# A feed-forward product by Strassen's seven quarter products, with its sums on GpSimd and VectorE

## The chip, the cores and the metric

The kernel runs on one core of a Trainium2 chip. A core has five engines, each with its own instruction queue that it works through in order: TensorE (PE in the profile; PEld is its weight load), VectorE (DVE), ScalarE (ACT), GpSimd (POOL) and SyncE (SP, which here only issues DMAs). PE reads its two operands from the on-chip memory SBUF and writes into PSUM, eight banks of 128 partitions by 512 float32 columns; DVE and ACT read PSUM, POOL does not. Engines wait for each other through semaphores. The metric is the device time of one execution in microseconds (us), lower is better; the median of several runs is compared.

## What is computed

The reference is one layer of a small perceiver with 8 sequences of 64 tokens (512 tokens, width 512) in float32. Three blocks follow each other, each of them added to its input:

```python
x = x + xattn(layernorm(x), ctx)          # 1601 context rows per sequence
x = x + attn(layernorm(x), ...)           # causal linear attention, 16 heads of 64, and a feed-forward block
x = x + ffn(layernorm(x), ...)            # 8 experts, each token uses 2 of them
```

The second block is the one that the change touches. Its end, with `b` for the input of the block:

```python
num, den = causal sums of phi(q) phi(k) v  and  phi(q) phi(k)
a  = num / (den + 1e-6)
y  = b + a @ wo                                       # 1024 -> 512
h2 = ln(y, g2, beta2)
y  = y + gelu(h2 @ w1 + b1, approximate=False) @ w2 + b2   # 512 -> 2048 -> 512
```

## The kernel before, in words

The 512 tokens are held as NT = 4 tiles of 128, the width of 512 as KC = 4 chunks of 128, and the inner width FF = 2048 as 16 blocks f of 128. The order of the instructions on every engine is the order in which the program calls them: it is written out by hand, and nothing reorders it. A float32 matmul appears in the trace as two passes, each with its own weight load. An engine that needs something that another engine has not finished waits, and with it everything behind it in its queue.

Weights come through a ring of 12 buffers of 1 MB in one fixed order (`stream`, `need`): a call of `need` also lets SP issue the loads up to six places ahead, and marks older ring buffers as free. The buffers are filled again when their last reader is done. The order after the attention weights is wo (2), then w1 and w2 in turn (4 of each), then the experts' weights.

PSUM has two groups of four banks: `mm_bank` for short products and `acc_bank` for long accumulations. During the feed-forward block the four `acc` banks hold the four accumulators of the second product (`mlp_0` to `mlp_3`), so all the rest goes through the four `mm` banks. Accesses of one bank by different engines are put in order one after the other.

The last part of the linear attention runs over j, eight pairs of heads. `attend_j(j)` gives two banks, each with the numerators in its left half and the denominators in its right half. `divide(j)` (L768 to L780) has ACT copy the denominators of both banks into the tile `rden` (L772), DVE take the reciprocal (L773) and DVE multiply it with the numerators into `a_t` (L775). `rden` has one buffer.

`output(t, js)` (L800) is the product with wo, into one bank for each token tile t. `join(t)` adds it to the residual `xin` on DVE (L833) and takes the statistics (L835 to L839), `normal(t)` makes the normalized rows `h2n` (L844, L845), and `turn_h2(t)` transposes them on PE into one bank (L850); its four chunks are then scaled and shifted into `h2_t`, by DVE (L858) and ACT (L854) in turn. `h2n` and `h2_t` are the two halves of the tile `v_sb`, under which name the profile shows them. Tile 3 is ready last, since the order of PE places its wo product last.

The first product of the feed-forward block, `hidden(f, tokens)` (L887), takes four matmuls (one for each chunk of the width) with 128 columns of w1 as the weights and the tokens as the moving operand. For f = 0 and 1 it is first done for the tokens of tiles 0 to 2 alone, and `turn_h2(3)` stands between these two. After that the loop over f (L917 to L925) does one whole `hidden(f)` with 512 moving columns, one gelu on ACT from the bank into a tile `hid` (L921), and for f from 1 to 8 the second product `mlp_out` (L908) of the block before, four matmuls. The second product of the last HELD = 8 blocks comes later, one token tile after the other (`last_chunks`), and is interleaved with the routing for the experts.

Between `hidden(1, ...)` and the loop, POOL gets eight additions of 128x512, two for each token tile: b2 to `xin` (L902), then `xin` to the residual `xs` (L903). The results are first read when the second product of tile 0 is complete (L956).

Of the kernel before, what the change touches and what calls it, by code (L numbers as in the profile page):

```python
# [31 lines left out]
FF = 2048  # L32
# [7 lines left out]
HELD = 8  # L40
# [8 lines left out]
def perceiver_kernel(  # L49
# [22 lines left out]
    nc = tc.nc  # L72
# [29 lines left out]
    mid = ctx.enter_context(ExitStack())  # L102
# [15 lines left out]
    half = H * DH // 2  # L118
# [4 lines left out]
    streamed, order, issued = {}, [], [0]  # L123
# [59 lines left out]
    def issue_to(n):  # L183

        while issued[0] < min(n, len(order)):
            key, src = order[issued[0]]
            if in_ring(key) and len(held) >= RING:
                if held[0] not in freed:
                    return
                held.pop(0)  # L190
            if key in places_of:
                t_ = places_of[key]
                nc.sync.dma_start(t_, src)
            elif key[0] == "tail":
                t_ = tails.tile([P, D], F32, tag="tail", name="_".join(str(k) for k in key))
                nc.sync.dma_start(t_, src)
            else:
                width = WIDTHS[key[2]] if key[0] == "ctxT" else 512
                t_ = ring.tile([P, 4, width], F32, tag="ring", name="_".join(str(k) for k in key))
                nc.sync.dma_start(t_, src)  # L200
                held.append(key)
            streamed[key] = t_
            issued[0] += 1

    def done(*keys):

# [26 lines left out]
    g1_c, beta1_c, g2_c, beta2_c = (col[:, i * KC : (i + 1) * KC] for i in range(4))  # L233
    b1_c = col[:, 4 * KC : 4 * KC + FF // P]
# [431 lines left out]
    xas.close()  # L666


    las = ctx.enter_context(ExitStack())
    la1 = las.enter_context(tc.tile_pool(name="la1", bufs=1))  # L670
    la2 = las.enter_context(tc.tile_pool(name="la2", bufs=2))
    if True:
        a_t = la1.tile([P, H * DH // P, B * S], F32, name="a_t")

# [92 lines left out]

        def divide(j, both):  # L768

            rden = la2.tile([P, 2, NT * S], F32, tag="rden", bufs=1, name=f"rden_{j}")  # L770
            for h in range(2):
                nc.scalar.activation(rden[:, h, :], both[h][:, NT * S :], AF.Identity, bias=tiny)  # L772
            nc.vector.reciprocal(rden, rden)  # L773
            for h in range(2):
                nc.vector.tensor_tensor(  # L775
                    a_t[:, j, :].rearrange("p (t h q) -> p t h q", t=NT, h=2)[:, :, h, :],
                    both[h][:, : NT * S].rearrange("p (t q) -> p t q", t=NT),
                    rden[:, h, :].rearrange("p (t q) -> p t q", t=NT),
                    ALU.mult,
                )  # L780
# [12 lines left out]
        wo_r = [need("wo", r) for r in range(2)]  # L793
        wo_banks = {}

        def output(t, js):
            if t not in wo_banks:
                wo_banks[t] = (mm_bank if t < 3 else acc_bank)(f"wo_{t}")
            for j in js:
                nc.tensor.matmul(  # L800
                    wo_banks[t],
                    a_t[:, j, t * P : (t + 1) * P],
                    wo_r[j // 4][:, j % 4, :],
                    start=(j == 0),
                    stop=(j == nj - 1),
                )
# [22 lines left out]
        h2n, h2_t = v_sb[:, :, :D], v_sb[:, :, D:]  # L829
# [12 lines left out]
        def normal(t, mv, std):  # L842
            rstd = small.tile([P, 1], F32, tag="rstd1", name=f"rstd_h2_{t}")
            nc.vector.reciprocal(rstd, std)  # L844
            nc.vector.tensor_scalar(h2n[:, t, :], xin[:, t, :], mv[:, 0:1], rstd, ALU.subtract, ALU.mult)  # L845

        def turn_h2(t):
            bank = mm_bank(f"tr_h2_{t}")
            for c in range(KC):
                nc.tensor.transpose(bank[:, c * P : (c + 1) * P], h2n[:, t, c * P : (c + 1) * P], ident)  # L850
            for c in range(KC):
                dst, part = h2_t[:, c, t * P : (t + 1) * P], bank[:, c * P : (c + 1) * P]
                if c % 2:
                    nc.scalar.activation(  # L854
                        dst, part, AF.Identity, scale=g2_c[:, c : c + 1], bias=beta2_c[:, c : c + 1]
                    )
                else:
                    nc.vector.tensor_scalar(  # L858
                        dst, part, g2_c[:, c : c + 1], beta2_c[:, c : c + 1], ALU.mult, ALU.add
                    )  # L860

        of = join(0), join(1)
        for t in range(2):
# [17 lines left out]
    def hidden(f, tokens):  # L881

        w = need("w1", f // 4)
        if f not in hid_banks:
            hid_banks[f] = mm_bank(f"hid_{f}")
        for c in range(KC):
            nc.tensor.matmul(  # L887
                hid_banks[f][:, tokens],
                w[:, c, (f % 4) * P : (f % 4 + 1) * P],
                h2_t[:, c, tokens],  # L890
                start=(c == 0),
                stop=(c == KC - 1),
            )

    hid_banks = {}

    hidden(0, slice(0, 3 * P))
    turn_h2(3)
    hidden(1, slice(0, 3 * P))

    for t in range(NT):
        nc.gpsimd.tensor_tensor(xin[:, t, :], xin[:, t, :], b2_bc, ALU.add)  # L902
# [4 lines left out]
    def mlp_out(t, f, hid):  # L907
        nc.tensor.matmul(  # L908
            acc[t],
            hid[:, t * P : (t + 1) * P],  # L910
            need("w2", f // 4)[:, f % 4, :],
            start=(f == 0),
            stop=(f == FF // P - 1),
        )

    hids = []
    nf = FF // P  # L917
    for f in range(nf):
        hidden(f, slice(3 * P, 4 * P) if f < 2 else slice(0, 4 * P))
        hid = mlp2.tile([P, B * S], F32, tag="hid", bufs=HELD + 1, name=f"hid_sb_{f}")  # L920
        nc.scalar.activation(hid, hid_banks[f], AF.Gelu, bias=b1_c[:, f : f + 1])  # L921
        hids.append(hid)
        if 0 < f <= nf - HELD:
            for t in range(NT):
                mlp_out(t, f - 1, hids[f - 1])  # L925

    warm = mlp.tile([P, 1], F32, name="warm")
    nc.scalar.activation(warm, eps, AF.Sqrt)
# [174 lines left out]
    t = NT - 1  # L1103
# [51 lines left out]
    bank = acc_bank("counts")  # L1155
# [636 lines left out]
```

## The time and the profile before

| | |
|---|---|
| median of 3 runs | 631.76 us (631.12 to 632.06) |
| the profiled execution | 631.35 us, its span 629.5 us, 1.85 us around it |
| PE busy | 613.7 us, 97% of the span |
| DVE, ACT, POOL busy | 166.5, 136.1, 64.9 us |
| first product, L887 | 144 passes, 56.6 us busy |
| second product, L908 | 112 passes, 51.0 us busy |
| last wo product to first late chunk of the second product | 278.01 to 362.13 us |

The times in the views below are microseconds from the start of the span. A group's line gives the line in the kernel, engine, operation, output and inputs, the shape, the number of instructions, then their busy time in us and the mean duration of one in ns, then the engine's idle time just before them with what ended it. A line of the timeline gives the start, the length, the engine, the line, the operation, how many instructions were merged into it, and in brackets how long the engine sat idle before it and what released it. Matmuls overlap: the distance between the starts of two passes is what one costs, and is less than its duration.

### The profile page before, as it was taken

What the parts mean: (1) busy time and instruction counts of PE and PEld (TensorE: products, weight loads), DVE (VectorE), ACT (ScalarE), POOL (GpSimd) and SP (SyncE); (2) the same over time, 40 slices, a digit from 0 to 9 for tenths busy, and PEclk for the clock granted to TensorE, in tenths of its full rate; (3) what the DMA queues carried; (4) which work ended last, traced back from release to release, by engine and by line L of the source; (5) the groups of instructions that cost most, each with busy time, mean ns of one, the idle gap of its engine ahead of it and who ended that gap; (6) DMA issues with size and microseconds to landing.
All of it is one profiled execution on the core that took longest, in us unless ns stands there. A gap on an engine that the chain in (4) does not pass through costs nothing. (4 is left out here: it accounts for less than half of the span.)

```text
span 629.5 us, 8757 instructions
## 1 busy us (share of the span) xinstructions
PE 613.7 (97%) x3572; PEld 350.2 (56%) x3572; DVE 166.5 (26%) x398; ACT 136.1 (22%) x260; POOL 64.9 (10%) x89
## 2 busy tenths in 40 slices
PE   8999999999999999999999999999999999999994
PEld 6543534344444454445444447967783767775793
DVE  4112414242302757870000026511311101011100
ACT  2241232130134354231101111301101101111110
POOL 4000000000000000050000003331310121301110
PEclk9999999999999999999999999999999999999998
DMA  8999999999713004030312121437890577785711
GB/s 336 421 418 417 419 419 417 419 419 413 295 59 99 35 2 134 2 135 0 128 31 109 68 100 67 172 94 252 299 352 0 178 291 274 295 328 152 290 19 17
DMA packets 23937, 131.81 MB, mean 209 GB/s; under 512 B 4372, under 2 KB 4372, under 8 KB 12488
## 3 DMA queue, kind: packets, MB, share of 16 engines
q1 hardware_dynamic: 19496, 122.36, 49.6%
q0 software_dynamic: 3280, 7.61, 5.0%
q10 hardware_dynamic: 1104, 1.07, 0.5%
q8 instruction: 38, 0.62, 0.4%
q14 instruction: 19, 0.16, 0.1%
HBM read 126.08 MB, written 4.94 MB: 208 GB/s over the span
## 5 line engine op out<-in xcount | busy, mean ns | idle before, releaser
L1289 PEld LDWEIGHTS up<-xgT,e_up 128*128 128x128 f32 x896 | 100.7, 192 | 4.5 <-ACT y_sb L1267 2.5
L1289 PE MATMUL up<-xgT,e_up 128*128 128x128 f32 x896 | 101.6, 275 | 1.0 <-PEq L1622 0.6
L1303 PE MATMUL y<-e_wo,mid 128*128 128x512 f32 (+1 forms) x144 | 58.8, 547 | 0.0
L887 PE MATMUL hid<-v_sb,w 128*128 128x512 f32 (+2 forms) x144 | 56.6, 545 | 0.0
L1255 DVE TENSOR_TENSOR mid<-up,act 128x256 f32<-128x256 f32 x38 | 16.1, 425 | 150.3 <-ACT act L1253 150.3
L908 PE MATMUL mlp<-w,hid_sb 128*128 128x512 f32 x112 | 51.0, 597 | 0.0
L458 PE MATMUL sc<-ctxT,pw_t 128*64 128x401 f32 (+1 forms) x256 | 46.6, 503 | 0.3 <-DMA ctxT<-in_ctx_T_dram 0.3
L519 PE MATMUL av<-ctx,eT 128*64 128x512 f32 x192 | 44.3, 595 | 0.0
L887 PEld LDWEIGHTS hid<-v_sb,w 128*128 128x128 f32 x144 | 26.1, 190 | 29.2 <-issue 26.8
L1253 ACT ACTIVATE act<-up 128x256 f32<-128x256 f32 x38 | 14.6, 384 | 119.6 <-PE up L1289 97.4
L1303 PEld LDWEIGHTS y<-e_wo,mid 128*128 128x128 f32 x144 | 25.7, 190 | 20.5 <-issue 17.8
L1268 POOL DMA_INDIRECT out_dram<-y_sb,dst_late x12 | 18.3, 1526 | 167.4 <-ACT y_sb L1267 97.6
L908 PEld LDWEIGHTS mlp<-w,hid_sb 128*128 128x128 f32 x112 | 20.7, 190 | 23.5 <-issue 23.4
L458 PEld LDWEIGHTS sc<-ctxT,pw_t 128*64 128x64 f32 x256 | 17.6, 136 | 27.6 <-issue 26.3
L902 POOL TENSOR_TENSOR xin<-xin,b_bc 128x512 f32<-128x512 f32 x4 | 5.1, 1265 | 265.6 <-DVE rstd_h L844 262.7
L800 PE MATMUL wo<-wo,a_t 128*128 128x512 f32 x64 | 29.5, 603 | 1.1 <-DVE a_t L775 1.1
L684 PE MATMUL wq<-h_t,wq 128*128 128x512 f32 x64 | 29.4, 602 | 0.0
L589 PE MATMUL v<-wv,h_t 128*128 128x512 f32 x64 | 29.1, 597 | 0.0
L684 PE MATMUL wk<-h_t,wk 128*128 128x512 f32 x64 | 28.8, 592 | 0.0
L519 PEld LDWEIGHTS av<-ctx,eT 128*64 128x64 f32 x192 | 14.7, 136 | 25.1 <-issue 23.1
L773 DVE RECIPROCAL rden<-rden 128x512 f32<-128x512 f32 x8 | 26.8, 3346 | 1.5 <-ACT rden L772 1.5
L921 ACT ACTIVATE hid_sb<-hid,col 128x512 f32<-128x512 f32 x16 | 11.0, 687 | 68.0 <-PE hid L887 68.0
(272 smaller groups left out, 611.8 us busy)
## 6 DMA issues: line engine op xcount, KB each, us to landing
e_up<-in_L_ffn_up_dram SPq DMA_DIRECT2D x32, 1024.0 KB, 5.3
ctx<-in_ctx_dram SPq DMA_DIRECT2D x24, 1024.0 KB, 15.7
ctxT<-in_ctx_T_dram SPq DMA_DIRECT2D x24, 802.0 KB, 13.9
e_wo<-in_L_ffn_wo_dram SPq DMA_DIRECT2D x16, 1024.0 KB, 9.7
w<-in_L_attn_w_dram SPq DMA_DIRECT2D x8, 1024.0 KB, 8.7
ctxT<-in_ctx_T_dram SPq DMA_DIRECT2D x8, 796.0 KB, 17.6
wv<-in_L_attn_wv_dram SPq DMA_DIRECT2D x2, 1024.0 KB, 14.0
wq<-in_L_attn_wq_dram SPq DMA_DIRECT2D x2, 1024.0 KB, 15.6
```

Of the source, the lines that this page charges most:

```text
L458: nc.tensor.matmul(sc[h * S : (h + 1) * S, :width], pw_t[:, c, (2 * t + h) * S : (2 * t + h + 1) * S], keys[h][:, c, :], start=(c == 0), s ...
L519: nc.tensor.matmul(av[h * S : (h + 1) * S, :], e_t[:, 4 * g + j, h * S : (h + 1) * S], rows[h][:, j, :], start=(g == 0 and j == 0), stop=F ...
L589: nc.tensor.matmul(bank, h_t[:, c, t * P : (t + 1) * P], wv_n[:, c, :], start=(c == 0), stop=(c == KC - 1))
L684: nc.tensor.matmul(bank, w[:, c, (j % 4) * P : (j % 4 + 1) * P], h_t[:, c, :], start=(c == 0), stop=(c == KC - 1),)
L773: nc.vector.reciprocal(rden, rden)
L800: nc.tensor.matmul(wo_banks[t], a_t[:, j, t * P : (t + 1) * P], wo_r[j // 4][:, j % 4, :], start=(j == 0), stop=(j == nj - 1),)
L887: nc.tensor.matmul(hid_banks[f][:, tokens], w[:, c, (f % 4) * P : (f % 4 + 1) * P], h2_t[:, c, tokens], start=(c == 0), stop=(c == KC - 1),)
L908: nc.tensor.matmul(acc[t], hid[:, t * P : (t + 1) * P], need("w2", f // 4)[:, f % 4, :], start=(f == 0), stop=(f == FF // P - 1),)
L1255: nc.vector.tensor_tensor(hid, bank[:, FQ:], act, ALU.mult)
L1268: nc.gpsimd.indirect_dma_start(out=out, out_offset=bass.IndirectOffsetOnAxis(ap=dst[:n, :], axis=0), in_=y_sb[:n, :], in_offset=None, boun ...
L1289: nc.tensor.matmul(bank[:, m * P : (m + 1) * P], up_of[q][:, c, m * P : (m + 1) * P], xg_t[c], start=(c == 0), stop=(c == KC - 1),)
L1303: nc.tensor.matmul(bank[:, :width], h_t[:, j * P : (j + 1) * P], w[:, 2 * (q % 2) + j, n * width : (n + 1) * width], start=(q + j == 0), s ...
```

## The change

Three things change.

First, the first feed-forward product. Two blocks f = 2i and 2i+1, the two halves of the width (chunks 0, 1 and 2, 3) and the two halves of the tokens (tiles 0, 1 and 2, 3) make a product of 2 by 2 quarters. Strassen's form (Winograd's variant) takes seven quarter products in the place of eight, with four sums of weights (`sum_weights(i)`: s1 to s4, on POOL) and four sums of tokens (`sum_tokens`: t1 to t4, once; token tiles 0 and 2 on POOL, token tiles 1 and 3 on DVE). A quarter product is two matmuls with 256 moving columns. The seven results are put together partly by accumulating in a bank, partly by six DVE instructions for each i that read a bank, and three gelu activations in the place of two. `sum_weights(0)` and `(1)` are called ahead of the wo product, the others one round ahead of their use.

In a round i the instructions on PE are: P1 and P2 into bank 0 (P1 is copied out by DVE before P2 accumulates on it), P5 and P3 into bank 1, P6, P7 and P4 into bank 2, each of them with a DVE read between the products. P4 of round i is called one round later. Ahead of the loop PE does P1(0), P1(1), P2(0), P2(1), the transposes of tile 3, P1(2) and P2(2).

Second, `rden` gets two buffers.

Third, `turn_h2` lets one engine scale a whole bank: ACT for tiles 0 and 1, DVE for tile 2; tile 3 is transposed into two banks of the `acc` group, ACT scaling the one and DVE the other.

```diff
+    sumw = mid.enter_context(tc.tile_pool(name="sumw", bufs=2))
+    def quarter(i, row, half):
+        w = streamed["w1", i // 2]
+        at = (2 * (i % 2) + row) * P
+        return w[:, 2 * half : 2 * half + 2, at : at + P]
+    def sum_weights(i):
+        s = wsums[i] = sumw.tile([P, 4, 2, P], F32, tag="sumw", name=f"sumw_{i}")
+        s1, s2, s3, s4 = (s[:, k] for k in range(4))
+        nc.gpsimd.tensor_tensor(s1, quarter(i, 1, 0), quarter(i, 1, 1), ALU.add)
+        nc.gpsimd.tensor_tensor(s2, s1, quarter(i, 0, 0), ALU.subtract)
+        nc.gpsimd.tensor_tensor(s3, quarter(i, 0, 0), quarter(i, 1, 0), ALU.subtract)
+        nc.gpsimd.tensor_tensor(s4, quarter(i, 0, 1), s2, ALU.subtract)
...
-            rden = la2.tile([P, 2, NT * S], F32, tag="rden", bufs=1, name=f"rden_{j}")
+            rden = la2.tile([P, 2, NT * S], F32, tag="rden", name=f"rden_{j}")
...
         wo_r = [need("wo", r) for r in range(2)]
+        for i in range(2):
+            sum_weights(i)
...
+        def sum_tokens(eng, tile):
+            t1, t2, t3, t4 = (ts[:, :, tile * P : (tile + 1) * P] for ts in tsum)
+            near, far = tokens(0, 0, tile), tokens(0, 1, tile)
+            eng.tensor_tensor(t1, far, near, ALU.subtract)
+            eng.tensor_tensor(t3, tokens(1, 1, tile), far, ALU.subtract)
+            eng.tensor_tensor(t2, t3, near, ALU.add)
+            eng.tensor_tensor(t4, tokens(1, 0, tile), t2, ALU.subtract)
...
-        turn_h2(0)
-        turn_h2(1)
+        turn_h2(0, [by_act])
+        turn_h2(1, [by_act])
         output(3, range(3, nj - 2))
-        turn_h2(2)
+        turn_h2(2, [by_dve])
...
-    hidden(0, slice(0, 3 * P))
-    turn_h2(3)
-    hidden(1, slice(0, 3 * P))
+    def first_products(i):
+        need("w1", i // 2)
+        for f in range(2 * i, 2 * i + 2):
+            hids[f] = mlp2.tile([P, B * S], F32, tag="hid", bufs=HELD + 1, name=f"hid_sb_{f}")
+        open_bank(i, 0)
+        product(i, 1, 0, quarter(i, 0, 0), tokens(0, 0), True)
+        nc.vector.tensor_copy(hids[2 * i + 1][:, :HT], sides[i, 0][:, :HT])
+    def second_products(i):
+        product(i, 2, 0, quarter(i, 0, 1), tokens(1, 0))
+        gelu(2 * i, hids[2 * i][:, :HT], sides[i, 0][:, :HT])
+    def fifth(i):
+        open_bank(i, 1)
+        product(i, 5, 1, wsums[i][:, 0], tsum[0], True)
+        even, odd = hids[2 * i], hids[2 * i + 1]
+        nc.vector.tensor_tensor(odd[:, HT:], sides[i, 1][:, :HT], odd[:, :HT], ALU.add)
...
+    def fourth(i):
+        product(i, 4, 2, quarter(i, 1, 1), tsum[3])
+        odd = hids[2 * i + 1]
+        nc.vector.tensor_tensor(odd[:, :HT], sides[i, 2][:, :HT], odd[:, :HT], ALU.add)
+        gelu(2 * i + 1, odd, odd)
+    sum_tokens(nc.gpsimd, 0)
+    for i in range(2):
+        first_products(i)
+    for i in range(2):
+        second_products(i)
+    turn_h2(3, [by_act, by_dve])
+    sum_tokens(nc.vector, 1)
+    first_products(2)
+    second_products(2)
     for t in range(NT):
         nc.gpsimd.tensor_tensor(xin[:, t, :], xin[:, t, :], b2_bc, ALU.add)
         nc.gpsimd.tensor_tensor(xs[:, t, :], xs[:, t, :], xin[:, t, :], ALU.add)
...
+    np_ = nf // 2
+    for i in range(np_):
+        if i > 2:
+            first_products(i)
+        if i + 1 < np_ and i + 1 not in wsums:
+            sum_weights(i + 1)
+        fifth(i)
+        if i > 0:
+            fourth(i - 1)
+        sixth(i)
+        if i > 2:
+            second_products(i)
+        third(i)
+        seventh(i)
+        if 0 < i <= (nf - HELD) // 2:
+            for f in (2 * i - 2, 2 * i - 1):
+                for t in range(NT):
+                    mlp_out(t, f, hids[f])
+    fourth(np_ - 1)
```

`sixth`, `third` and `seventh` have the form of `fifth`: a product into the bank named above, then one DVE addition that reads it; `third` also has the gelu of the right half of block 2i.

More of the change, by code (lines that the diff above doesn't have):

```diff
@@ L671, in perceiver_kernel @@
     la2 = las.enter_context(tc.tile_pool(name="la2", bufs=2))
+    wsums = {}
+    def quarter(i, row, half):
[9 more added lines that the diff above has]
+        nc.gpsimd.tensor_tensor(s4, quarter(i, 0, 1), s2, ALU.subtract)
     if True:
@@ L845, in normal, with by_act @@
             nc.vector.tensor_scalar(h2n[:, t, :], xin[:, t, :], mv[:, 0:1], rstd, ALU.subtract, ALU.mult)
[L847 to L860, printed above, removed]
+        def by_act(dst, part, scale, shift):
+            nc.scalar.activation(dst, part, AF.Identity, scale=scale, bias=shift)
@@ new lines, in by_dve, with turn_h2 @@
+        def by_dve(dst, part, scale, shift):
+            nc.vector.tensor_scalar(dst, part, scale, shift, ALU.mult, ALU.add)
+        def turn_h2(t, scaled):
+            n = KC // len(scaled)
+            for i, scale in enumerate(scaled):
+                bank = (acc_bank if t == NT - 1 else mm_bank)(f"tr_h2_{t}_{i}")
+                for c in range(i * n, (i + 1) * n):
+                    part = bank[:, (c - i * n) * P : (c - i * n + 1) * P]
+                    nc.tensor.transpose(part, h2n[:, t, c * P : (c + 1) * P], ident)
+                for c in range(i * n, (i + 1) * n):
+                    part = bank[:, (c - i * n) * P : (c - i * n + 1) * P]
+                    scale(h2_t[:, c, t * P : (t + 1) * P], part, g2_c[:, c : c + 1], beta2_c[:, c : c + 1])
@@ new lines, in perceiver_kernel, with tokens @@
+        HT = B * S // 2
+        tsum = [h2n[:, k, :].rearrange("p (c q) -> p c q", c=2) for k in range(3)]
+        tsum.append(sumw.tile([P, 2, HT], F32, tag="sumh", bufs=1, name="sumh"))
+        def tokens(half, side, tile=None):
+            at = slice(side * HT, (side + 1) * HT) if tile is None else slice(side * HT + tile * P, side * HT + tile * P + P)
+            return h2_t[:, 2 * half : 2 * half + 2, at]
+        def sum_tokens(eng, tile):
[5 more added lines that the diff above has]
+            eng.tensor_tensor(t4, tokens(1, 0, tile), t2, ALU.subtract)
@@ L879, in perceiver_kernel @@
     mlp2 = mid.enter_context(tc.tile_pool(name="mlp2", bufs=2))
[L881 to L892, printed above, removed]
-            )
-    hid_banks = {}
@@ L897, in perceiver_kernel, with product @@
-    hidden(0, slice(0, 3 * P))
-    turn_h2(3)
-    hidden(1, slice(0, 3 * P))
+    sides, hids = {}, {}
+    nf = FF // P
+    def product(i, k, bank, weights, rows, first=False):
+        bank = sides[i, bank]
+        for c in range(2):
+            nc.tensor.matmul(
+                bank[:, :HT],
+                weights[:, c, :],
+                rows[:, c, :],
+                start=(first and c == 0),
+                stop=(c == 1),
+                skip_group_check=True,
+            )
@@ new lines, in open_bank, with gelu @@
+    def open_bank(i, k):
+        sides[i, k] = mm_bank(f"side_{i}_{k}")
+    def first_products(i):
[5 more added lines that the diff above has]
+        nc.vector.tensor_copy(hids[2 * i + 1][:, :HT], sides[i, 0][:, :HT])
+    def gelu(f, dst, src):
+        nc.scalar.activation(dst, src, AF.Gelu, bias=b1_c[:, f : f + 1])
@@ new lines, in second_products, with sixth @@
+    def second_products(i):
[6 more added lines that the diff above has]
+        nc.vector.tensor_tensor(odd[:, HT:], sides[i, 1][:, :HT], odd[:, :HT], ALU.add)
+    def sixth(i):
+        open_bank(i, 2)
+        product(i, 6, 2, wsums[i][:, 1], tsum[1], True)
+        even, odd = hids[2 * i], hids[2 * i + 1]
+        nc.vector.tensor_tensor(even[:, HT:], sides[i, 2][:, :HT], odd[:, :HT], ALU.add)
@@ new lines, in third, with seventh @@
+    def third(i):
+        product(i, 3, 1, wsums[i][:, 3], tokens(1, 1))
+        even = hids[2 * i][:, HT:]
+        nc.vector.tensor_tensor(even, sides[i, 1][:, :HT], even, ALU.add)
+        gelu(2 * i, even, even)
+    def seventh(i):
+        product(i, 7, 2, wsums[i][:, 2], tsum[2])
+        odd = hids[2 * i + 1]
+        nc.vector.tensor_tensor(odd[:, HT:], sides[i, 2][:, :HT], odd[:, HT:], ALU.add)
+    def fourth(i):
+        product(i, 4, 2, quarter(i, 1, 1), tsum[3])
+        odd = hids[2 * i + 1]
+        nc.vector.tensor_tensor(odd[:, :HT], sides[i, 2][:, :HT], odd[:, :HT], ALU.add)
+        gelu(2 * i + 1, odd, odd)
@@ L914, in mlp_out @@
         )
[L916 to L925, printed above, removed]
+    np_ = nf // 2
[17 more added lines that the diff above has]
+    fourth(np_ - 1)
     warm = mlp.tile([P, 1], F32, name="warm")
```

## The prediction

> **What bounds the kernel now.** I read the page's engine shares first, then the groups, then who waits for whom between 150 and 300 us, then the timeline around the change.
>
> ```profile
> PE 613.7 (97%) x3572; PEld 350.2 (56%) x3572; DVE 166.5 (26%) x398; ACT 136.1 (22%) x260; POOL 64.9 (10%) x89
> L887 PE MATMUL hid<-v_sb,w 128*128 128x512 f32 (+2 forms) x144 | 56.6, 545 | 0.0
> L908 PE MATMUL mlp<-w,hid_sb 128*128 128x512 f32 x112 | 51.0, 597 | 0.0
> ```
>
> TensorE is busy for 97% of the span: time goes only where PE passes go, or where a new wait makes PE idle. The waits of PE in this part are two:
>
> ```profile
> PE wo L800 <- DVE a_t L775: 1.1, 1, 1.1
> PE tr_h L850 <- DVE v_sb L845: 0.8, 1, 0.8
> ```
>
> The pitch of the passes, from the timeline (start, length, count):
>
> ```profile
> 338.10 24.20 PE L887 MATMUL hid<-v_sb,w 128*128 128x512 f32 x56
> ...
> 613.73 7.07 PE L1303 MATMUL y<-e_wo,mid 128*128 128x256 f32 x32
> ```
>
> A pass of 512 columns lasts 0.592 us (a group's mean) and 56 take 24.20, so the pitch is (24.20 - 0.592)/55 = 0.429 us. A pass of 256 lasts 0.379, and 32 take 7.07: pitch (7.07 - 0.379)/31 = 0.216. Halving the columns halves the price almost exactly; the weight load of 0.190 us still fits under it.
>
> **Part 1, passes.** Removed: 112 passes of 512 columns, 16 of 384 (8 take 2.74 us less the overlap, 0.32 each) and 16 of 128 (0.114): 112 x 0.429 + 16 x 0.32 + 16 x 0.114 = 48.0 + 5.1 + 1.8 = 55.0 us. Added: 8 rounds x 7 products x 2 matmuls x 2 passes = 224 passes x 0.216 = 48.3 us. Gain 6.7 us, all on PE's path. A check of the method: from 278.01 (the end of the wo product) to 362.13 (first late chunk) before has 55.0, 0.5 for four transposes, 64 passes of L908 x 0.429 = 27.5, and 0.8 idle: 83.8 of the measured 84.1.
>
> **Part 2, the denominators.**
>
> ```profile
> 255.17 0.84 ACT L772 ACTIVATE rden<-nd,tiny 128x256 f32<-128x256 f32 x2 [4.29 <-DVE a_t L775]
> 260.30 0.84 ACT L772 ACTIVATE rden<-nd,tiny 128x256 f32<-128x256 f32 x2 [4.29 <-DVE a_t L775]
> 261.17 3.35 DVE L773 RECIPROCAL rden<-rden 128x512 f32<-128x512 f32 x1 [0.99 <-ACT rden L772]
> ...
> 265.44 1.98 PE L800 MATMUL wo<-wo,a_t 128*128 128x512 f32 x4 [1.08 <-DVE a_t L775]
> ```
>
> ACT waits twice for the one buffer, so DVE sits idle 0.33 and 0.99 us before the last two reciprocals. With two buffers ACT has copied while DVE still divides; the last `a_t` comes 1.3 us earlier, more than PE's 1.08 us of waiting: gain 1.1, at least 0 (no work is added) and at most 1.1, since PE has no other idle time there.
>
> **Part 3, up to the first new products.** ACT alone scales tiles 0 and 1: eight of 0.405 (two take 0.81 in L854's rows), from about 273.3 to 276.6, before PE needs them at 278.01: 0. DVE is no longer held up by ACT in tile 2, so `join(3)` starts when its bank is complete, at 277.58 + 0.59 + 0.14 = 278.3 in the place of 278.74. `sum_weights(0)` and `(1)` are eight POOL additions of 256 columns, 0.75 us each by a line through 1.27 (512, L902) and 0.32 (32 columns, L291); POOL is idle from 8 to 270 us, so 0. The w1 loads are issued from 153 us on and land 5 to 13 us later. If that cover were gone, the 6 us would stand in front of P5(0).
>
> **Part 4, the first stall.** These are the rows before of tile 3's normalization:
>
> ```profile
> 270.69 1.58 DVE L845 TENSOR_SCALAR v_sb<-xin,mv_h,rstd_h 128x512 f32<-128x512 f32 x1
> 270.73 1.27 POOL L902 TENSOR_TENSOR xin<-xin,b_bc 128x512 f32<-128x512 f32 x1 [262.67 <-DVE rstd_h L844]
> 272.07 1.34 POOL L903 TENSOR_TENSOR xs<-xs,xin 128x512 f32<-128x512 f32 x1
> ...
> 278.74 0.68 DVE L833 TENSOR_TENSOR xin<-wo,xin 128x512 f32<-128x512 f32 x1
> ...
> 280.99 0.55 DVE L845 TENSOR_SCALAR v_sb<-xin,mv_h,rstd_h 128x512 f32<-128x512 f32 x1
> 281.59 0.66 PE L850 MATMUL tr_h<-ident,v_sb 128*128 128x128 f32 x4 [0.83 <-DVE v_sb L845]
> ```
>
> P2(0) accumulates on the bank that DVE's copy of P1(0) reads, and that copy is queued on DVE behind `join(3)` and `normal(3)`. From 278.3 the chain of 2.80 us (278.74 to 281.54) ends at 281.1; the copy takes 0.42 (256 columns, as L775). P2(0) starts at about 281.56. PE has only P1(0) and P1(1) before it: 278.01 + 8 x 0.216 = 279.74. Stall 1.8 us, where before it was 0.8. To this comes a wait that the first row shows: an L845 that met a POOL addition took 1.58 in the place of 0.55. After the change POOL is busy from 277.4 (when two chunks of tile 2 are scaled) with four sums, 3.0 us, and then eight additions of 1.3, up to 291, so `normal(3)` at 280.6 meets it for certain. Between 0 and 1.03 us more; I take 0.5.
>
> **Part 5, the second stall.** After P2(0), P2(1), the transposes and P1(2) PE needs P2(2), which waits for the copy of P1(2), and that is queued behind DVE's four `sum_tokens`. Counted without any delay: P2(1) ends 283.3, transposes 283.8, P1(2) 284.64. ACT has its gelu of P2(1) first (to 283.9), then two scalings of 0.405: 284.7. Then DVE's four sums, 1.44 us at the 0.34 to 0.37 pitch of L775's pairs, 286.2; the copy, 286.6; P2(2) at 286.7. Stall 2.0 us. Unknown: no row before has a DVE instruction with both inputs in SBUF beside a POOL one. By the nearest row, L845, each could wait for a whole POOL addition. Ends: 0, and 4 x 1.27 = 5.1 us. I take one wait of half an addition, 0.7, because another L845, at 274.44, kept its 0.55 while POOL worked without a break from 270.73 to 278.7.
>
> [...]
>
> **Part 6, the rounds.** Every DVE read lasts 0.42 and starts about 0.17 after its product; between a product and the next one on its bank stands at least one other, 0.86 us, so 0.27 are to spare. DVE does six reads in 6.0 us of PE work (2.5 busy), ACT 1.6; `sum_weights(i+1)` takes 3.0 and has eight products, 6.9 us. Last gelu: six matmuls x 0.858 = 5.1 us of late chunks come before it is needed. Cost 0; if the 0.27 is too little by 0.4 in every round, 3.2. POOL's additions for the residual end at 291 and are first read at 369. `need("w1", 1)` is asked for some rounds earlier; PE waits for no weights in 150 to 300 us, nor in the expert part, so SP's queue has cover and the whole gain is carried to the end.
>
> **The sum**, against the profiled execution's 631.35 (span 629.5 and 1.85 around it), which is 0.41 below the median: -6.7 passes, -1.1 denominators, -0.8 old stall, +2.3 first stall (1.8 + 0.5), +2.7 second (2.0 + 0.7) = -3.6, or 627.75; on the median's footing 628.15. I say 628.0.
>
> **The rivals.**
> - No port wait: stalls 1.8 + 2.0; -4.8, 626.6. For it: the L845 row of 274.44. Against it: the 1.58 row, and POOL working throughout.
> - Slower: DVE's four sums and POOL's additions take turns, one whole addition before each sum. Stalls 1.8 + 0.5 and 2.0 + 5.1 less about 0.8 for the first, partial wait: 8.6, which makes the sum 0 (631.4). PE then stands idle some 6 us in one piece. The only rows of PE after an idle start are the program's first 24 passes, 4.87 us, pitch (4.87 - 0.39)/23 = 0.195 where the same shape later has 0.114; such a restart would lose up to 24 x 0.08 = 2 us. That gives 631.4 to 633.4, with the full 1.03 in the first stall 634. It decides from a total stall of 8.6 us on. For it: the 1.58 row, and that POOL's next row started (272.07) before DVE had finished (272.27). Against it: DVE's sums need no semaphore between them.
> - The rounds are not free: 0.4 lost in each, -3.6 + 3.2 = 631.0, slower if it is 0.45 or more.
> - Passes of 256 columns at the weight load's pace: the 7.07 us row speaks against it; at 0.24 (L1111's passes among others' work) the gain would fall by 5.4 and the time be 633.1.
>
> [...]
>
> **How the numbers follow.** One wait or two: 0.40. No wait: 0.20. Turns: 0.28. Rounds: 0.08. Slow passes: 0.04. About 0.2%, 1.3 us, is what a measurement can tell. Faster holds the first two and a little of the turns, 0.62; same the lower part of the turns and half of the rounds, 0.13; slower the rest, 0.25. The range starts below the case of no wait (626.6 less 0.6, for the old idle time of 0.3 that the check of part 1 leaves over and the scatter of the runs) and leaves out the worst of the turns: 626.0 to 633.2. The likeliest case alone has 626.6 (one end of the unknown waits) to 629.5.
>
> **What would show it.** L887's successors as 224 passes of 256 columns at 0.216 pitch. No wait of L800 for L775. Two idle stretches of PE, before P2(0) and P2(2), released by DVE's copies: 2.3 and 2.7 us. DVE's four sums at 0.42 each, or stretched to 1.3 and more beside POOL's L902 and L903 rows; that stretch would prove the turns and make me wrong. PE idle inside the rounds, released by DVE or ACT, would prove that they are not free. Wrong also, to the better side, if the copies are not what PE waits for.

## The result, and the profile after

The changed kernel takes 636.10 us (median of 6 runs, 635.89 to 640.23), the kernel before 631.61 us in the same series (631.12 to 632.06). The two medians differ by 4.49 us. The ratio of all runs on record, a seventh of 637.16 us among them, is 1.0086, with an interval of 1.0063 to 1.0108: the change makes the kernel 0.7 to 0.9% slower, where 628.0 was forecast. All times given below are of executions at the usual clock; one of a later kernel, 720.66 us at a mean clock of 0.85, is left out of them. The profiled execution of the changed kernel is the slowest of the six, 640.23 us with a span of 638.3 us; times in its views have to be read against the 631.35 us and 629.5 us of the profile before.

The page's engine shares and the groups of the new product, after:

```profile
PE 613.1 (96%) x3652; PEld 369.8 (58%) x3652; DVE 190.8 (30%) x448; ACT 138.8 (22%) x270; POOL 90.5 (14%) x125
L927 PE MATMUL side<-v_sb,sumw 128*128 128x256 f32 x128 | 32.7, 398 | 0.0
L927 PE MATMUL side<-v_sb,w 128*128 128x256 f32 x64 | 17.2, 399 | 8.6 <-DVE hid_sb L946 8.6
```

PE is as busy as before although its passes are shorter in sum, because some of them ran at half clock, as shown below. In front of the new product stand 8.6 us of idle time; before the change, L887 had none and the transposes between its passes had 0.8. Who waits for whom between 200 and 450 us, after (total, number of times, longest):

```profile
PE side L927 <- DVE hid_sb L946: 8.6, 2, 6.0
PE up L1443 <- PEq L1722: 2.9, 1, 2.9
PE side L927 <- DVE hid_sb L976: 0.5, 1, 0.5
```

The wait of the wo product for the last `a_t` and that of the transposes for tile 3 are gone. In their place stand the two waits for DVE's copies that the prediction had named, one at the end of the rounds, and one that it had not: PE waits for its own sequencer (PEq) at L1722, a branch of the first expert (`few_of[e] == 1`). PE's timeline at the two copies:

```profile
276.50 1.89 PE L927 MATMUL side<-v_sb,w 128*128 128x256 f32 x8
280.94 1.97 PE L927 MATMUL side<-v_sb,w 128*128 128x256 f32 x8 [2.56 <-DVE hid_sb L946]
...
290.26 2.08 PE L927 MATMUL side<-v_sb,w 128*128 128x256 f32 x4 [6.05 <-DVE hid_sb L946]
292.13 5.19 PE L927 MATMUL side<-v_sb,sumw 128*128 128x256 f32 x14
```

The first stall is 2.56 us (2.3 predicted), the second 6.05 (2.7 predicted). And four passes that took 1.03 us without a stall ahead of them take 2.08 behind the second one; 14 more take 5.19. Why the second stall is so long can be read from the timelines of DVE and of POOL over the same time (L896 to L899 are DVE's four sums of tokens, L995 and L996 POOL's additions, L946 the copy):

```profile
278.95 1.51 DVE L865 TENSOR_SCALAR v_sb<-xin,mv_h,rstd_h 128x512 f32<-128x512 f32 x1
...
284.15 1.51 DVE L896 TENSOR_TENSOR v_sb<-v_sb 128x256 f32<-128x256 f32 x1
285.59 1.48 DVE L897 TENSOR_TENSOR v_sb<-v_sb 128x256 f32<-128x256 f32 x1
287.10 1.37 DVE L898 TENSOR_TENSOR v_sb<-v_sb 128x256 f32<-128x256 f32 x1
288.50 1.37 DVE L899 TENSOR_TENSOR sumh<-v_sb 128x256 f32<-128x256 f32 x1
289.80 0.41 DVE L946 COPY hid_sb<-side 128x256 f32<-128x256 f32 x1
```

```profile
284.13 1.26 POOL L995 TENSOR_TENSOR xin<-xin,b_bc 128x512 f32<-128x512 f32 x1
285.46 1.32 POOL L996 TENSOR_TENSOR xs<-xs,xin 128x512 f32<-128x512 f32 x1
286.75 1.44 POOL L995 TENSOR_TENSOR xin<-xin,b_bc 128x512 f32<-128x512 f32 x1
288.27 1.32 POOL L996 TENSOR_TENSOR xs<-xs,xin 128x512 f32<-128x512 f32 x1
```

Each sum ends 0.27 to 0.29 us after the POOL addition beside it (285.66 and 285.39, 287.07 and 286.78, 288.47 and 288.19, 289.87 and 289.59): DVE gets one short turn after each whole addition, four times. The sums take 5.7 us in the place of the 1.44 counted. What happened to the passes behind the stall shows in the granted clock, the share of full speed at which PE was allowed to run. Columns: the stretch, its length, PE's busy time and passes, the granted clock, DMA share and rate:

```profile
285.00:288.00 3.00, 0.00 (x0) 1.00 0.00 0
288.00:290.00 2.00, 0.00 (x0) 0.84 0.00 0
290.00:291.00 1.00, 0.74 (x2) 0.50 0.00 0
...
295.00:296.00 1.00, 1.00 (x4) 0.50 0.00 0
296.00:297.00 1.00, 1.00 (x6) 0.91 0.00 0
```

From 290.26 to 296.1 PE works at half its clock, which loses half of 5.8 us, 2.9. With that the first late chunk of the second product starts at 365.55 us in the place of 362.13, 3.4 later. The second loss of the profiled execution is at the branch; the same place before and after:

```profile
421.22 3.64 PE L1341 MATMUL up<-e_up,xgT 128*32 128x512 f32 x32 [0.45 <-ACTq L1620]
```

```profile
427.12 6.39 PE L1443 MATMUL up<-e_up,xgT 128*32 128x512 f32 x32 [2.92 <-PEq L1722]
```

The wait is 2.5 us longer, and here too the clock falls (0.50 from 426 to 432 us), so that the same 32 passes take 6.39 us in the place of 3.64: 5.2 us in all.

### The profile page after: what moved, and what is told of

Its sections match the earlier page's. It is cut to its first block, busy times and chain, and to the rows that moved or that the text cites. A ratio compares the mean times of both kernels' runs of the same rounds, so it can differ in the third digit from the quotient of the medians.

```text
span 638.3 us, 9028 instructions
## 1 busy us (share of the span) xinstructions
PE 613.1 (96%) x3652; PEld 369.8 (58%) x3652; DVE 190.8 (30%) x448; ACT 138.8 (22%) x270; POOL 90.5 (14%) x125
## 3 DMA queue, kind: packets, MB, share of 16 engines
q10 hardware_dynamic: 1104, 1.07, 0.5%
## 5 line engine op out<-in xcount | busy, mean ns | idle before, releaser
L685 POOL TENSOR_TENSOR sumw<-w 128x256 f32<-128x256 f32 x8 | 5.8, 726 | 207.7 <-PE v L589 159.7
L927 PE MATMUL side<-v_sb,sumw 128*128 128x256 f32 x128 | 32.7, 398 | 0.0
L927 PEld LDWEIGHTS side<-v_sb,sumw 128*128 128x128 f32 x128 | 25.9, 202 | 4.4 <-issue 0.5
L927 PE MATMUL side<-v_sb,w 128*128 128x256 f32 x64 | 17.2, 399 | 8.6 <-DVE hid_sb L946 8.6
```

What stands on the lines that cost most here:

```text
L927: nc.tensor.matmul(bank[:, :HT], weights[:, c, :], rows[:, c, :], start=(first and c == 0), stop=(c == 1), skip_group_check=True,)
```

## The experiments

Two theories stood against each other. Theory A: the sums on DVE wait for POOL's reads, the long idle time that follows lowers PE's clock, and with POOL out of the way the calculation of the prediction holds. Theory B: the order of DVE's queue (copies behind the sums) costs most of it, or the passes and rounds themselves are dearer than counted, and POOL is a bystander.

**POOL's eight additions moved behind the sums of weights of round 3.**

```diff
-    for t in range(NT):
-        nc.gpsimd.tensor_tensor(xin[:, t, :], xin[:, t, :], b2_bc, ALU.add)
-        nc.gpsimd.tensor_tensor(xs[:, t, :], xs[:, t, :], xin[:, t, :], ALU.add)
...
         if i + 1 < np_ and i + 1 not in wsums:
             sum_weights(i + 1)
+        if i == 2:
+            residual(range(NT))    # the same eight additions
         fifth(i)
```

> The changed kernel with one difference: POOL's eight additions for the residual stand behind sum_weights(3), in the round i = 2, so they no longer run beside DVE's four sums of tokens. Theory (DVE's two-input sums and POOL's additions take turns on something both need): the four sums take 0.42 us each in the place of 1.37 to 1.51, L865 for tile 3 keeps 0.55 in the place of 1.51, the stall before P2(0) falls from 2.6 to about 1.6 us and the one before P2(2) from 6.0 to about 2.0, and with no idle time over 3 us the granted clock stays at 1.00 in the part that showed 0.50. Time: 636.1 less 1.0, less 4.0, less 2.9 (5.8 us at half clock) = 628.2 us. Rival (the sums are slow by themselves, by their strided shape or their place in the queue): the sums stay near 1.4 us, the stall stays near 6, and the time stays at 636.

Measured: 631.33 us, ratio to the kernel before 0.9993 (0.9983 to 1.0002). In the timeline of DVE the sums have their 0.42 us again, and PE's stalls are 1.59 and 2.00, to 0.2 us the 1.8 and 2.0 that the prediction had counted without a meeting:

```profile
283.38 0.42 DVE L896 TENSOR_TENSOR v_sb<-v_sb 128x256 f32<-128x256 f32 x1
...
284.63 0.42 DVE L899 TENSOR_TENSOR sumh<-v_sb 128x256 f32<-128x256 f32 x1
```

```profile
280.17 1.97 PE L927 MATMUL side<-v_sb,w 128*128 128x256 f32 x8 [1.59 <-DVE hid_sb L946]
...
285.44 2.01 PE L927 MATMUL side<-v_sb,w 128*128 128x256 f32 x4 [2.00 <-DVE hid_sb L946]
```

The additions were the cause of the stretched sums. But the time is 3 us above what was expected. The traced execution, 632.73 us, is the slowest of the ten (629.07 to 632.73), so a usual one may lose less of what follows. Two things were missing from the calculation. The clock still fell behind the second stall, of 2.00 us (mean 0.66 from 285 to 290 us; 2.01 us for four passes), a loss of about 1.7 us (0.34 of 5); the first late chunk is at 359.52, 2.6 earlier than before. The 3 us of idle time in the expectation were the author's estimate; no run shows such a limit. And the wait at the branch is there, 2.63 us, with the clock down behind it.

**Filler for the second stall.** Additions where the change puts them, and 22 matmuls of 128x128 into an unused bank ahead of P2(2), so that PE isn't idle in one piece.

```diff
     first_products(2)
+    filler = acc_bank("filler")
+    for _ in range(22):
+        nc.tensor.matmul(filler[:, :P], ident, ident, start=True, stop=True)
     second_products(2)
```

> The changed kernel with 22 matmuls of 128x128 on the identity into a spare bank, just ahead of P2(2), where PE stands idle for 6.0 us; they add no work to the result. Theory (part of the loss is that PE's clock is granted at 0.50 for some microseconds after that idle time): the filler takes 44 passes x 0.114 = 5.0 us of the idle 6.0, the granted clock stays at 1.00, the products after it keep the pitch of 0.216 us, and the time falls by half of the 5.8 us that ran at half clock: 636.1 - 2.9 = 633.2 us. DVE's sums stay at 1.4 us each. Rival (the clock has no part in it, the difference is all in the waits): no change, 636.

Measured: 632.30 us, 1.0012 (1.0002 to 1.0021). The sums still take 1.52, 1.49, 1.37 and 1.37 and PE's time up to P2(2) is the same, but the clock is 1.00 throughout, and the first late chunk is at 362.71 in the place of 365.55: 2.84 us, which is the loss by the clock behind the second stall, measured by itself. The timeline shows the next passes at the full pace, 20 in 4.48 us:

```profile
284.09 5.08 PE L994 MATMUL filler<-ident 128*128 128x128 f32 x44
290.32 1.13 PE L927 MATMUL side<-v_sb,w 128*128 128x256 f32 x4 [1.16 <-DVE hid_sb L946]
291.29 4.48 PE L927 MATMUL side<-v_sb,sumw 128*128 128x256 f32 x20
```

The wait at the branch is 0.4 to 0.5 us in this kernel, which was not expected; more of that below.

**Additions later and the copies ahead of the sums.** As the first experiment, and `first_products(2)` called right after those of rounds 0 and 1, so that DVE's copy of P1(2) no longer stands behind its sums.

```diff
-    for i in range(2):
+    for i in range(3):
         first_products(i)
...
     sum_tokens(nc.vector, 1)
-    first_products(2)
     second_products(2)
```

> POOL's additions behind sum_weights(3) as in the run before, and P1(2) with its copy called right behind P1(0) and P1(1), so that DVE has the copy of P1(2) ahead of its sums and PE has three products in the place of two before it needs the copy of P1(0). If both stalls come from the copies' place in DVE's queue: the first stall is 0.9 us less than with the additions moved alone, about 0.8, and the second is 0.5 or less (P5(0) needs only t1, 0.4 us behind the scaling of tile 3). Time 628.2 - 0.8 - 1.5 = about 626. If PE then only waits at the next place, for the DVE read of P5(0) that is queued behind the four sums, the gain is under 1 us: 627.5 or more.

Measured: 627.16 us, 0.9936 (0.9921 to 0.9951). The stalls are 0.64, 0.51 and 0.52 us, the clock is 1.00 throughout, and the first late chunk is at 355.30, 6.8 earlier than before. The wait at the branch is 2.70 us, here without a fall of the clock (the 32 passes take 3.64):

```profile
280.00 1.99 PE L927 MATMUL side<-v_sb,w 128*128 128x256 f32 x8 [0.64 <-DVE hid_sb L946]
...
283.80 4.56 PE L927 MATMUL side<-v_sb,sumw 128*128 128x256 f32 x20 [0.51 <-DVE v_sb L896]
...
416.64 3.64 PE L1445 MATMUL up<-e_up,xgT 128*32 128x512 f32 x32 [2.70 <-PEq L1724]
```

With additions and copies both moved, the loss turns into a gain.

**The same copy order with the additions left in place.**

```diff
-    for i in range(2):
+    for i in range(3):
         first_products(i)
...
-    first_products(2)
     second_products(2)
     for t in range(NT):
         nc.gpsimd.tensor_tensor(xin[:, t, :], xin[:, t, :], b2_bc, ALU.add)
```

> The changed kernel with P1(2) and its copy called right behind P1(0) and P1(1), and POOL's additions left where they are. The sums stay at 1.4 us each and end about 5.7 us after they start. If the copy's place alone made the second stall, P2(2) no longer waits and PE only waits for t1 and t2 where P5(0) and P6(0) need them: some 1.5 and 2.5 us, and the DVE read of P5(0), queued behind t4, is late by another 2, so that the 6.0 us come back in two or three pieces of 2, in sum 4 to 5. If PE can work on in between, the sum of the stalls after the transposes is under 2.

Measured: 633.96 us, one run. The sums take 0.43, 1.49, 1.37 and 1.37, PE waits 1.59 before P2(0), then 0.51 and 1.71 for sums and 0.55 for the DVE read of P5(0) that is queued behind them, and the clock is 0.74 from 290 to 295. The order alone shortens the second stall from 6.05 to 2.8 in three pieces and leaves the turns as they are, but for the first sum: it began 0.03 us ahead of POOL's addition, kept its 0.43, and the addition took 1.52. Theory B explains a part, A the larger one: by the medians and this one run, moving the additions alone gave back 4.8 us, the order alone 2.1, both together 8.9.

**Is it POOL's work, or its reading?** The additions are moved as in the first experiment, and in their old place POOL writes zeros into a scratch tile.

```diff
+    idle_rows = mlp.tile([P, 1216], F32, name="idle_rows")
+    for _ in range(2 * NT):
+        nc.gpsimd.memset(idle_rows, 0.0)
```

> The changed kernel with POOL's eight additions moved behind sum_weights(3), as in the first of the runs, and eight POOL memsets of 128x1216 on a scratch tile in their old place, so that POOL is as busy beside DVE's sums as with the additions, but only writes and reads nothing. Theory A (what they take turns on is the reading side: DVE's second input and POOL's inputs): the four sums take 0.42 us each, the stall before P2(2) is near 2.0 us. Theory B (any POOL instruction that is under way keeps DVE's two-input sums out): the sums take 1.3 us or more, the stall is near 6. [...]

Measured: 633.49 us, one run. POOL writes without a break from 279.12 to 288.57, and the sums of DVE beside it keep their time:

```profile
285.75 0.42 DVE L896 TENSOR_TENSOR v_sb<-v_sb 128x256 f32<-128x256 f32 x1
286.08 0.42 DVE L897 TENSOR_TENSOR v_sb<-v_sb 128x256 f32<-128x256 f32 x1
286.53 0.43 DVE L898 TENSOR_TENSOR v_sb<-v_sb 128x256 f32<-128x256 f32 x1
286.99 0.42 DVE L899 TENSOR_TENSOR sumh<-v_sb 128x256 f32<-128x256 f32 x1
```

So, as far as one run shows it, it is not that POOL is busy that holds up the sums, but that it reads: 0.42 to 0.43 us beside the zeros, 1.37 to 1.51 beside the additions. The normalization L865 took 1.33 us beside the zeros, against 0.55 in the first experiment, where POOL stood idle at that time: it was held up by the writing too. With it the first stall became 2.38 us, and the clock fell behind it already (eight passes in 3.23 us): P1(2) starts 2.45 us later than in the first experiment, which is about what this run is slower (2.2).

**The denominators alone**, on the kernel before:

```diff
-            rden = la2.tile([P, 2, NT * S], F32, tag="rden", bufs=1, name=f"rden_{j}")
+            rden = la2.tile([P, 2, NT * S], F32, tag="rden", name=f"rden_{j}")
```

> The kernel before with two buffers for the denominators and nothing else. The trace of the changed kernel shows no wait of L820 for L793 and the end of the wo product 1.5 us earlier. If that comes from the two buffers: the wait of 1.08 us of PE is gone and the time is 631.6 - 1.1 = 630.5 us. If it comes from ACT scaling whole banks, the time stays at 631.6.

Measured: 629.97 us, 0.9973 (0.9962 to 0.9983), and the first late chunk at 360.80, 1.33 earlier. The part is worth 1.3 to 1.7 us, and scaling a bank by one engine costs nothing on PE's path up to the end of the wo product (276.68 here, 276.50 after the change).

**The branch.** The wait was 2.4 to 2.9 us in the kernels with the change's number of instructions, and 0.4 to 0.5 in the one with 44 matmul passes more (the filler), whatever else was in them. One theory is that the place of the branch in PE's instruction stream is what counts; the other, that the wait comes from what the other engines or the transfers do at that time. By the first, 88 instructions more (44 passes and 44 weight loads) anywhere ahead of it must take the wait away, and some 160, as the change adds (80 more passes), must bring it into the kernel before. Three kernels got more matmuls on the identity at the program's start:

```diff
-    for _ in range(NIDLE):
+    for _ in range(9):
         nc.tensor.matmul(idle_bank[:, :P], ident, ident, start=True, stop=True)
+    for _ in range(25):    # 47 on the kernel before
+        nc.tensor.matmul(idle_bank[:32, :8], ident[:, :32], ident[:, :8], start=True, stop=True)
```

The additions later, the copies first, and 88 instructions more:

> The version with both moves (additions later, P1(2)'s copy first), and 88 more instructions in PE's queue at the very start of the program: the 12 matmuls that warm PE up become 9, with 25 tiny ones behind them (32 columns of weights, 8 moving), while PE waits for its first input anyway. Theory (the wait of 2.7 us of L1445 for L1724 at the first of the experts' branches, which is in the traces of the changed kernel and of three of its variants but not in the one with the 88 filler instructions, depends on where the branch lies in PE's stream of instructions): the wait is 0.5 us again, the clock after it stays at 1.00, and the time falls by 2 to 3 us, to about 625.0. Rival (it comes from what the other engines or the transfers do at that time): the wait stays, the time stays at 627.

Measured: 625.53 us, 0.9907 (0.9890 to 0.9924), with 0.45 us at the branch. These matmuls run over the program's first transposes, which start at 7.50 in the place of 6.96; by the first P1 0.1 us of that is left in the trace (276.71 against 276.61).

The changed kernel and 88 instructions more:

> The changed kernel itself with the same 88 instructions in PE's queue at the start. The trace's own stage times make the loss up to the late chunks 3.4 us, which would be 635.0; the time measured is 636.1. If the rest is the branch: its wait is 0.5 us again and the time is 634.9. If not: 636.1.

Measured: 634.56 us (four runs, 633.66 to 636.63, the slowest of them traced), 1.0044 (1.0028 to 1.0060), with 0.45 us at the branch and the 32 passes there back at 3.64:

```profile
426.28 3.64 PE L1445 MATMUL up<-e_up,xgT 128*32 128x512 f32 x32 [0.45 <-ACTq L1724]
```

This is 1.5 us less than the changed kernel, but it is no clean measure of the branch: the first P1 starts 1.9 us later (278.43), the second stall is 4.52, and the clock fell behind the first stall already, of 2.55 us, which it did not do behind the 2.56 us of the changed kernel. What the run shows is the wait at the branch, which is gone with the change's work untouched.

The kernel before and 176 instructions more:

> The kernel before with 176 instructions more at the start of PE's queue (9 matmuls of 128 columns and 47 tiny ones in the place of 12), about as many as the change adds there, and nothing of the change. If the position of the branch in PE's stream is the whole cause of its wait, the kernel before now shows it too: L1341's successor waits 2.4 to 2.9 us for the sequencer at the first branch in the place of 0.45, and 4 to 5 us in sum are lost with the clock, beside 1 to 2 us at the start. If the change's own work is needed for it, the wait stays at 0.45.

Measured: 634.86 us, one run. The wait is now in the kernel before, with no part of the change in it; the clock does not fall behind it:

```profile
423.71 3.64 PE L1343 MATMUL up<-e_up,xgT 128*32 128x512 f32 x32 [1.87 <-issue]
```

So it is the number of instructions ahead of the branch, not the work of the change. This kernel lost 3.1 us to the kernel before: 1.4 are the wait, 1.0 a later start (the wo product ends at 279.05), and 0.6 are not accounted for. Counted from the kernel before, the wait is 0.4 to 0.5 us at 0 and at 248 instructions more, 2.4 to 2.9 us at 160 and 1.87 at 176; why at these counts is not shown. The pages count the packets of an instruction queue (packets, MB, share; after and before):

```profile
q8 instruction: 40, 0.66, 0.4%
```

```profile
q8 instruction: 38, 0.62, 0.4%
```

There are also 40 in the first and the third experiment, which have the long wait, 38 in the kernel with two `rden` buffers and 39 in the one with the filler, which have the short one. By the DMA records of the traces of the changed kernel and the kernel before, one such packet is under way at the branch in both. In the changed kernel it lands at 425.27, and PE goes on 1.85 us later, at 427.12; in the kernel before PE goes on at 421.22, before it has landed (421.63). From these times the author's estimate is that the long wait is one for instructions; no trace shows what its sequencer waits for.

**All of it together, with the added instructions in PE's idle time.** Additions later, copies first, and the 88 instructions as 11 small matmuls before P2(0) and 11 before P5(0), where PE would wait.

```diff
...
+    tiny_matmuls(11)
     for i in range(2):
         second_products(i)
...
+        if i == 0:
+            tiny_matmuls(11)
         fifth(i)
```

> The version with both moves, and the 88 instructions for the position of the branch not at the start of the program but where PE stands idle in any case: 11 tiny matmuls (32 columns of weights, 8 moving) ahead of P2(0), where it waits 0.64 us, and 11 ahead of P5(0), where it waits 0.51. At 30 ns a pass they fit (22 passes, 0.66 us, each). If the branch's wait goes with the position alone, it is 0.45 again, and the time is 624.5 with less scatter than with the instructions at the start, which held up the first transposes by 0.5 to 1.5 us. If the tiny matmuls cost more than the idle time holds, 625.5.

Measured: 624.99 us (624.89 to 625.11), 0.9893 (0.9877 to 0.9910): 1.07% faster than the kernel before and 1.7% faster than the changed one. In the waits of PE both copies and the sequencer are gone. The 22 small passes take 0.79 and 0.80 us, 36 ns each, where the expectation has 30; the timeline:

```profile
279.35 0.86 PE L991 MATMUL filler<-ident 128*32 128x8 f32 x22
...
283.36 0.86 PE L991 MATMUL filler<-ident 128*32 128x8 f32 x22
...
355.68 9.60 PE L1008 MATMUL mlp<-w,hid_sb 128*128 128x512 f32 x22
...
414.77 3.64 PE L1454 MATMUL up<-e_up,xgT 128*32 128x512 f32 x32 [0.45 <-PE xgt L1356]
```

## Why the prediction was wrong

The forecast had the wrong sign. By its own steps:

- **Passes (−6.7): right to 0.4.** In the last experiment the new passes are hardly disturbed: from 276.66 to 355.68 are 79.0 us, less 1.6 for the two fillers, 0.4 for the transposes, 27.5 for the second product and 0.5 for the wait at the end of the rounds, which leaves 49.0 for 224 passes (48.3 predicted). The same account of the kernel with two `rden` buffers gives 55.3 for the old ones. The gain is 6.3.
- **Denominators (−1.1): right**, 1.3 by the timeline; the prediction's "at most 1.1" was a little too tight.
- **The old stall (−0.8): right**, it is gone.
- **First stall (2.3): right**, 2.56. The 1.8 counted without a meeting were 1.59 when the additions were out of the way; the 0.5 taken for the meeting was 1.0. The two misses partly cancel, so some of the agreement is luck.
- **Second stall (2.7): this is the step that failed.** Its 2.0 without a meeting were exact (2.00 in the first experiment). The term "one wait of half an addition, 0.7" was 4.0. The prediction chose it because one L845, at 274.44, had kept its 0.55 us beside a busy POOL. In the trace of before that row began 0.2 us before the end of POOL's addition (273.37 to 274.63), and the addition after it took 1.40 us in the place of some 1.27:

```profile
273.37 1.26 POOL L902 TENSOR_TENSOR xin<-xin,b_bc 128x512 f32<-128x512 f32 x1
...
274.44 0.55 DVE L845 TENSOR_SCALAR v_sb<-xin,mv_h,rstd_h 128x512 f32<-128x512 f32 x1
...
274.71 1.40 POOL L903 TENSOR_TENSOR xs<-xs,xin 128x512 f32<-128x512 f32 x1
```

The likely reading is that this row met the end of a turn, so that its time was no sign of free passage. The four sums all began within 0.4 us after POOL's next addition had begun, and each ended after it. The row of 1.58 was the nearer one: beside the additions the sums took 1.37 to 1.51 us and L865, with one tensor input, 1.51, against 0.42 to 0.43 and 0.55 with the additions moved. The prediction's first rival speaks of a "port wait"; no run shows a port, and what the runs showed are these times. The other steps:

- **The restart of the clock: priced in the rival, and only there.** It was bounded by 2 us and measured as 2.9 (2.84 by the filler); for the rows that it was priced from, the program's first passes, the profile shows a clock of 1.00. No term of the likeliest case had one, and yet the clock fell even with stalls of 1.59 and 2.00 us.
- **"The whole gain is carried to the end": false.** What was looked at were waits for data; the change also lengthened PE's instruction stream ahead of a branch. The longer wait there is worth 2.2 us between the two kernels that differ in little else (627.16 and 624.99).
- **The rounds at no cost: right** but for one wait of 0.5 us at their end.

With the measured terms the sum up to the first late chunk is −6.3 − 1.3 − 0.8 + 2.56 + 6.05 + 2.9 + 0.5 = +3.6, and the timeline has +3.4. The medians differ by 4.5, which leaves 1.1 for the branch, though it cost 5.2 in the profiled execution and 2.2 between the two kernels just named. Only the slowest of the runs of the changed kernel has a trace. The others have a mean clock of 0.989 to 0.991 against its 0.986 (the kernel before: 0.995 to 0.997), so they lost less to the clock, but where is not recorded: how the 4.5 of a usual run divide between the stalls with their clock and the branch stays open.

The rival "Slower: turns" named the mechanism, the place and the order of it; its total of 8.6 us for the two stalls is what was measured. It was given 0.28 and priced at 631.4 to 634; it came to 636.1 because the clock cost 2.9 in the place of 2 at most, and because of the branch.

## What to carry to other kernels

Before sums are put on VectorE, look at what GpSimd reads from SBUF at that time: here a two-input instruction of 0.4 us beside GpSimd's additions took as long as a whole addition, 1.4 us, and moving eight additions that nobody was waiting for gave back 4.8 us by itself. A stall of TensorE is not paid at its length alone: idle times of 2.4 us and more, or of 1.6 and 2.0 us with 3.3 us of work between, lowered its clock for the next few us in some of these kernels (0.50 for 5.8 us of work behind the 6.05 us, a mean of 0.66 over 5 us behind the 2.4 and behind the 1.6 and 2.0), while three pieces of 0.5 to 0.6 us did not (1.00). Filler where the wait can't be removed gave back 2.8 us. And in a kernel with branches the number of instructions ahead of a branch can change a wait there, here by 1.4 to 2.5 us; it is worth a look at the wait there before a small loss is put down to the edit.

## What was not expected of the hardware

- The clock fell after idle times of very different lengths: 6.05 us (0.50 from 290.26 to 296.1), 2.55 and 2.38 us in one piece (the eight passes behind them took 2.92 and 3.23 us), and 1.59 and 2.00 us with 3.3 us of work between (a mean of 0.66 from 285 to 290), while 2.56 us in the changed kernel and 2.55 in the one with the filler did nothing (1.00, the eight passes in 1.97 us). The same idle time gave both outcomes, so its length alone does not settle it; what does is not shown.
- The branch of the first expert costs PE 0.45 us or 1.9 to 2.9 us, by its place in the instruction stream, and the clock may fall behind it too: it did with waits of 2.4, 2.63 and 2.92 us (the 32 passes took 5.34 and 6.39 us behind the last two, in the place of 3.64; with the first the line's 96 passes took 672 ns on the mean, in the place of 595), and did not with 1.87, 2.6 and 2.70.
- The normalization on VectorE (L865), with one large input, took 1.33 us beside GpSimd's writing of zeros, against 0.55 alone, while the sums with two inputs kept their 0.42 beside the same writing (one run). Beside GpSimd's additions both kinds were held up, L865 to 1.51 us and the sums to 1.37 to 1.51: which kind is held up depends on what GpSimd does.
